# Row maxima of attention scores: a pair of key blocks through a difference, a relu on ScalarE and one sum-and-maximum on VectorE

## The chip, the cores and the metric

The kernel runs on one NeuronCore of a Trainium2 chip. Its engines work side by side, each through its own queue in order: TensorE (PE: matrix products, written to PSUM), VectorE (DVE), ScalarE (ACT), GpSimd (POOL, which reads and writes SBUF alone) and SyncE (SP, which issues DMAs). Engines wait for one another through semaphores. The metric is the time of one execution on the device in microseconds (us); less is better.

## The reference

One pre-norm decoder layer over `x` of 2 x 2048 tokens x 512 features, float32. The part that matters here is self-attention with 16 heads of 32 features:

```python
x = x + _L0_attn_ref(_layernorm(x, axis=-1), W_q, W_k, W_v, W_o)
x = x + _L0_xattn_ref(_layernorm(x, axis=-1), ctx_1024, ctx_1024)   # 77 context rows, gelu between two products
x = x + _L0_ffn_ref(_layernorm(x, axis=-1), weights, scale, bias)   # weights by their sign, scale, bias, clip

# in _L0_attn_ref:
Q = apply_rope(proj(W_q), pos, inv_freq)
K = apply_rope(proj(W_k), pos, inv_freq)
V = proj(W_v)
scores = jnp.einsum('bhqd,bhkd->bhqk', Q, K) / jnp.sqrt(jnp.float32(DK))
attn = jax.nn.softmax(scores, axis=-1)
out = jnp.einsum('bhqk,bhkd->bhqd', attn, V)
```

## The kernel before

For each of the two batches `project_batch` makes queries, keys and values, then `Attention.run` walks the attention, and `after_attention` does the rest of the layer for a finished block of 512 queries. `after_attention` is a generator: `background` takes small pieces of it and places them between the steps of the attention (and of the next batch's projection).

**Tiling of the attention.** Features lie on partitions: a group `g` is four heads of 32 rows each. Keys are held in four blocks of 512 (`self.k[0..3]`), queries in four blocks too. A *unit* `u` is 256 queries of one group: 32 units a batch. A unit has eight *steps* i = 0 to 7; step `t = 8 u + i` is the loop variable of `run` (L805). In each step every head of the group handles two chunks of 128 keys (L634: step i takes block i mod 4, its first half of two chunks for i < 4, its second half after that).

**Scores twice.** The exponentials need each query's maximum over all 2048 keys. It is found beforehand: `maxima` (L523) multiplies 128 queries by one block of 512 keys into a PSUM tile `ps` of 128 x 512, queries on partitions, and `reduce` takes the largest of each row with a VectorE reduce (L552) into one element of `mx`, laid out [chunk of queries, head, key block]. One unit's maxima take eight indices (2 chunks of queries x 4 key blocks), and they run 11 steps (`AHEAD`) ahead of the step that carries them. `split_maxima` reduces `mx` over the four blocks, negates it and splits it in three bfloat16 parts (VectorE once, then POOL); `turn_maxima` transposes these on VectorE and sends them through DRAM into `mrow`, as rows. At a unit's start `lower` (L644) puts the negated maximum into the four `st` tiles, and `scores` (L663) adds the products of keys and queries, keys on partitions. For that the `st` tile is not begun anew in every step: to get from one key block to the next, the product with the *difference* of two blocks, `self.dk[kb] = k[kb] - k[kb - 1]`, is added (L660). These differences are made by POOL at the start of a batch (`key_steps`, L600): group 0 at once, groups 1 to 3 as background work.

**One step** (L805 to L843) comes in two halves, heads (0, 1) and heads (2, 3). In the first half TensorE forms maxima products of heads 2 and 3 for step t + 11, interleaved with the score products of heads 0 and 1; ScalarE takes the exponentials of heads 0 and 1 (`pw`, L828); POOL adds their two chunks (`sm`, L830); VectorE reduces the two `ps` tiles. The second half is the same with the pairs of heads exchanged. Then `gather` calls `collect`, for the step before: the products of `pw` and values (`weigh`, L679) and of `sm` and ones (`total`, L693) go to a PSUM tile `acc`, and `acc` is added to the running `num` by VectorE (L712). In two steps of each unit part of that goes otherwise: in step 1 ScalarE copies the values part of `acc` to a new `num` (L716) while VectorE adds the sums part to the previous unit's `num` (L712, 128 x 64), which is then complete, and `divide` takes its reciprocal (L735) and, over the following steps, spreads and multiplies it. In step 2 ScalarE copies the sums part (L721) and VectorE adds the values part.

**Order and buffers.** `run` is under a schedule written by hand for PE, DVE, ACT and POOL: each engine's instructions stand in program order. PSUM has two pools of four buffers. `ps_t` holds the four `st` tiles. `ps_s` holds, in turn, the four `ps` tiles of a step and its `acc`, so five tiles go round in four buffers, and each takes the one that the tile four places earlier has given up: `acc` that of the same step's first `ps` (head 2), and head 1's `ps` that of the `acc` before. Background work takes its PSUM tiles from `ps_s` too while attention runs.

Of the kernel before, what the change touches and what calls it, by code (L numbers as in the profile page):

```python
# [9 lines left out]
F32 = mybir.dt.float32  # L10
F32R = mybir.dt.float32r
BF16 = mybir.dt.bfloat16
AF = mybir.ActivationFunctionType
ALU = mybir.AluOpType
AX = mybir.AxisListType

P = 128
# [4 lines left out]
BLK = 512  # L22
NB = S // BLK
# [6 lines left out]
PART = HQ // SPLIT  # L30
STEPS = NCH // 2
AHEAD = STEPS + 3
SCALE = 1.0 / math.sqrt(DK)
EPS = 1e-5
MAX_VAL = 100.0
# [4 lines left out]
def decoder_layer(  # L40
# [16 lines left out]
    nc = tc.nc  # L57
# [9 lines left out]
    ps_t = ctx.enter_context(tc.tile_pool(name="ps_t", bufs=4, space=bass.MemoryType.PSUM))  # L67
    ps_s = ctx.enter_context(tc.tile_pool(name="ps_s", bufs=4, space=bass.MemoryType.PSUM))
    nums = ctx.enter_context(tc.tile_pool(name="nums", bufs=2))


    def tokens(rows, ch):
# [138 lines left out]
    def project_batch(b, ahead, att, xnt, angles, wk, wq, wv):  # L211
# [15 lines left out]
        def values(ch, xnt, pool=None):  # L227
            pv = (pool or ps_s).tile([P, D], F32, tag="t" if pool else "s", name="pv")
            times(pv, xnt, wv)
            keep_values(ch, pv)  # L230

        def keep_values(ch, pv):
            v = kvq.tile([P, D], F32, tag=f"v{ch}", name=f"v_{b}_{ch}")
            nc.scalar.copy(v, pv)
            att.v.append(v)
# [63 lines left out]
        keep_values(ch - 1, pv)  # L299
        att.lead(AHEAD, 8)  # L300
        values(ch, xnt, ps_t)
# [207 lines left out]
    class Attention:  # L509
        def __init__(self, b):  # L510
            self.b = b
            self.q, self.k, self.v = [], [], []
            self.units = [(qb, g, hf) for qb in range(NB - 1) for g in range(ND) for hf in range(2)]
            self.units += [(NB - 1, g, hf) for hf in range(2) for g in range(ND)]
            self.mx = {}
            self.mrow = {}
            self.num = {}
            self.due = []
            self.st = {}
            self.rows = [slice(h * DK, (h + 1) * DK) for h in range(4)]  # L520


        def maxima(self, n, heads, between=None):  # L523
            u, i = divmod(n, STEPS)
            if u >= NU:
                if between:
                    between()
                return None
            qb, g, hf = self.units[u]
            qc, kb = divmod(i, NB)  # L530
            if u not in self.mx:
                self.mx[u] = small.tile([P, 2, 4, NB], F32, tag="mx", name="mx")
            q0 = hf * HQ + qc * P
            tiles = []
            for h in heads:
                pool, tag = (ps_t, "t") if len(heads) == 4 and h == 3 else (ps_s, "s")
                ps = pool.tile([P, BLK], F32, tag=tag, name="ps")
                nc.tensor.matmul(  # L538
                    ps,
                    self.q[qb][self.rows[h], g, q0 : q0 + P],  # L540
                    self.k[kb][self.rows[h], g, :],
                    start=True,
                    stop=True,
                )
                tiles.append((h, ps))
                if between and h == heads[0]:
                    between()
            mx = self.mx[u]

            def reduce():  # L550
                for h, ps in tiles:
                    nc.vector.tensor_reduce(mx[:, qc, h, kb : kb + 1], ps, AX.X, ALU.max)  # L552

            return reduce

# [44 lines left out]
        def key_steps(self):  # L600
            self.dk = [None] + [
                const.tile([P, ND, BLK], F32, tag=f"w{n}", name=f"dk{n}") for n in "kqv"
            ]
            self.wrap = None

            def differences(g):
                for kb in range(1, NB):
                    nc.gpsimd.tensor_sub(
                        self.dk[kb][:, g, :], self.k[kb][:, g, :], self.k[kb - 1][:, g, :]
                    )  # L610
                    yield False

            def others():
                for g in range(1, ND):
                    for _ in differences(g):
                        for _ in range(4):
                            yield False

            for _ in differences(0):
                pass  # L620
            queue.append(others())
# [141 lines left out]
        def open_block(self, kb):  # L763
            for n in range(AHEAD):
                if n % NB == kb:
                    self.due.append((n, (0, 1, 2, 3)))
# [10 lines left out]
        def run(self):  # L777
# [8 lines left out]
            def gather():  # L786
                nonlocal before
                if prev is not None or before is not None:
                    end = self.collect(prev, before)
                    if end is not None:  # L790
                        ends.append(end)
                before = prev
# [12 lines left out]
            for t in range(NU * STEPS):  # L805
                u, i = divmod(t, STEPS)
                if t == NU * STEPS - AHEAD:
                    free.append(True)
# [9 lines left out]
                for heads, others in (((0, 1), (2, 3)), ((2, 3), (0, 1))):  # L818
                    if i == 0:
# [3 lines left out]
                    reduce = self.maxima(  # L823
                        t + AHEAD, others, lambda: self.scores(u, i, heads, 0)
                    )
                    self.scores(u, i, heads, 1)
                    for h in heads:
                        nc.scalar.activation(pw[:, h], self.st[h], AF.Exp, scale=SCALE)  # L828
                    hs = slice(heads[0], heads[1] + 1)
# [6 lines left out]
                gather()  # L836
                if (t + AHEAD) % STEPS == 0 and u + 1 < NU:
                    self.turn_maxima(u + 1)
                if (t + AHEAD) % STEPS == STEPS - 1 and u + 1 < NU:
                    self.split_maxima(u + 1)  # L840
# [78 lines left out]
```

## Time and profile before

| | us |
|---|---|
| median of 3 runs | 2534.59 (2534.11 to 2536.28) |
| the profiled execution | 2535.18 |
| its span, first to last instruction | 2533.3 |

Busy time and number of the groups that the change touches or that stand beside them:

| line, engine, what | count | busy us | mean ns |
|---|---|---|---|
| L552 VectorE, reduce 128 x 512 to 128 x 1 | 2048 | 1268.1 | 680 |
| L828 ScalarE, exponential 128 x 512 | 2048 | 1062.8 | 603 |
| L830 POOL, sum 128 x 512 | 1024 | 1283.7 | 1274 |
| L712 VectorE, `acc` into `num` (three widths) | 512 | 227.2 | 444 |
| L716 ScalarE, copy of `acc`, 128 x 256 | 64 | 23.9 | 374 |
| L735 VectorE, reciprocal 128 x 64 | 64 | 35.4 | 553 |
| L168 VectorE, statistics of a row | 96 | 65.3 | 684 |

How to read what follows. A group's line gives line of the kernel, engine, operation and tiles. A timeline's line gives start, duration (both in us from the span's start), engine, line, operation, how many of them in a row are merged, and in brackets how long the engine was idle before and what ended that idle time. A line of waits gives who waited for whom, the total in us, how often, and the longest. The chain is followed back from the last instruction to whatever released each one. Durations of instructions in a row overlap: four exponentials of 0.60 us follow one another in 2.07 us. The ends of products are modelled, so a busy TensorE need not be at its peak.

### The profile page before, as it was taken

The page shows a single profiled execution, that of the slowest core. Times are in us where ns is not written, and L with a number is a line of the kernel's source. Part 1 is how long each engine was busy: PE and PEld are TensorE (multiplying, and loading weights), DVE is VectorE, ACT ScalarE, POOL GpSimd, SP SyncE. Part 2 cuts the span into 40 slices and gives each one's busy share as a digit, 9 for nine tenths or more (in the row PEclk, how much of TensorE's full clock was granted, in tenths as well). Part 3 has the DMA queues.
Part 4 walks back from the last instruction along what each step waited for, and adds up shares of the span by engine and source line. Part 5 has one row for each costly group of instructions (what it writes and reads, how often), then busy time and mean ns, then how long its engine had stood idle before and what let it go on. Part 6 is the DMA issues. An engine that isn't in the chain of part 4 may idle for free.

```text
span 2533.3 us, 89869 instructions
## 1 busy us (share of the span) xinstructions
PE 2472.2 (98%) x39268; PEld 1658.7 (65%) x39268; DVE 1835.2 (72%) x3891; ACT 1268.2 (50%) x2457; POOL 1754.6 (69%) x1925
## 2 busy tenths in 40 slices
PE   8999999999999999999999999999999999999898
PEld 4446777666766676666654467776677666766675
DVE  4447888787878787876444488886878787878665
ACT  2113666555656564654521156665556555645463
POOL 2326888678867886787743279785788678867882
PEclk9999999999999999999999999999999999999999
DMA  4000000001000000000211000000000001000100
GB/s 150 21 21 2 3 4 3 3 3 32 8 3 3 27 12 3 3 28 19 73 30 34 9 3 4 3 4 3 11 28 3 3 3 36 3 3 3 36 4 18
DMA packets 37048, 41.87 MB, mean 17 GB/s; under 512 B 19350, under 2 KB 19862, under 8 KB 36656
## 3 DMA queue, kind: packets, MB, share of 16 engines
q1 hardware_dynamic: 36656, 36.14, 4.7%
q8 instruction: 308, 5.05, 0.8%
q14 instruction: 84, 0.69, 0.1%
HBM read 27.23 MB, written 8.90 MB: 14 GB/s over the span
## 4 chain that ended last, share of the span: by engine, by line
PE 88%; DVE 5%; POOL 3%; DMA 2%; ACT 1%; issue 1%; SPq 0%; POOLq 0%; ACTq 0%
PE ps L538 21%; PE acc L679 18%; PE st L663 15%; PE acc L693 8%; PE pk L214 4%; PE pq L214 4%; PE po L446 4%; PE pv L214 4%; DVE mx L552 2%; PE pf L424 2%; POOL sm L830 2%; PE st L644 1%; PE ptqk L222 1%; PE po L472 1%; PE pt L377 1%; DVE st L168 1%
## 5 line engine op out<-in xcount | busy, mean ns | idle before, releaser
L830 POOL TENSOR_TENSOR sm<-pw 128x512 f32<-128x512 f32 x1024 | 1283.7, 1274 | 410.9 <-ACT pw L828 408.0
L828 ACT ACTIVATE pw<-st 128x512 f32<-128x512 f32 x2048 | 1062.8, 603 | 777.1 <-PE ps L538 576.8
L552 DVE TENSOR_REDUCE mx<-ps 128x1 f32<-128x512 f32 x2048 | 1268.1, 680 | 219.2 <-PE ps L538 218.4
L538 PE MATMUL ps<-k,q 32*128 32x512 f32 x4096 | 1054.1, 624 | 0.4 <-DVE mx L552 0.4
L679 PE MATMUL acc<-pw,v 128*32 128x256 f32 x8192 | 551.9, 387 | 5.5 <-DVE mx L552 4.5
L538 PEld LDWEIGHTS ps<-k,q 32*128 32x128 f32 x4096 | 374.4, 185 | 97.4 <-issue 23.9
L679 PEld LDWEIGHTS acc<-pw,v 128*32 128x32 f32 x8192 | 214.9, 109 | 282.0 <-DVE mx L552 180.9
L693 PEld LDWEIGHTS acc<-sm,ones 128*32 128x32 f32 x16384 | 305.0, 110 | 89.5 <-POOL sm L830 1.4
L693 PE MATMUL acc<-sm,ones 128*32 128x64 f32 x16384 | 323.1, 219 | 1.1 <-POOL sm L830 1.1
L712 DVE TENSOR_TENSOR num<-acc,num 128x320 f32<-128x320 f32 (+2 forms) x512 | 227.2, 444 | 101.8 <-PE acc L693 59.3
L663 PE MATMUL st<-q,dkq 32*128 32x256 f32 x2048 | 261.5, 390 | 0.0
L663 PE MATMUL st<-q,dkv 32*128 32x256 f32 x2048 | 255.4, 390 | 0.0
L663 PE MATMUL st<-q,dkk 32*128 32x256 f32 x2048 | 252.6, 388 | 0.0
L250 POOL TENSOR_TENSOR r<-r 128x512 f32<-128x512 f32 x64 | 81.2, 1270 | 151.4 <-DVE r L249 151.4
L663 PEld LDWEIGHTS st<-q,dkq 32*128 32x128 f32 x2048 | 169.8, 184 | 9.3
L663 PEld LDWEIGHTS st<-q,dkk 32*128 32x128 f32 x2048 | 165.1, 184 | 10.0 <-ACT pw L828 0.4
L663 PEld LDWEIGHTS st<-q,dkv 32*128 32x128 f32 x2048 | 164.9, 185 | 8.9 <-ACT pw L828 0.2
L663 PE MATMUL st<-q,k 32*128 32x256 f32 x1024 | 145.7, 401 | 0.0
L663 PE MATMUL st<-q,wrap 32*128 32x256 f32 x1024 | 129.8, 390 | 0.0
L168 DVE BATCH_NORM_STATS2 st<-x 128x6 f32<-128x512 f32 x96 | 65.3, 684 | 84.1 <-DMA x<-in_x_dram 83.9
L223 ACT COPY q<-ptqk 128x512 f32<-128x512 f32 x32 | 18.8, 586 | 203.2 <-PE ptqk L222 203.2
L214 PE MATMUL pk<-wk,xnt 128*128 128x512 f32 x256 | 117.7, 603 | 2.1 <-ACT xnt L206 2.1
(118 smaller groups left out, 2164.3 us busy)
## 6 DMA issues: line engine op xcount, KB each, us to landing
x<-in_x_dram SPq DMA_DIRECT2D x64, 256.0 KB
out_dram<-x SPq DMA_DIRECT2D x32, 256.0 KB
mrow<-rows SPq DMA_DIRECT2D x496, 0.8 KB
wv<-in_wv_t_dram SPq DMA_DIRECT2D x2, 1024.0 KB
wk<-in_wk_t_dram SPq DMA_DIRECT2D x4, 256.0 KB
wq<-in_wq_t_dram SPq DMA_DIRECT2D x4, 256.0 KB
wo<-in_wo_t_dram SPq DMA_DIRECT2D x1, 1024.0 KB
wf<-in_wf_t_dram SPq DMA_DIRECT2D x4, 256.0 KB
```

What stands on the lines that cost most here:

```text
L168: nc.vector.bn_stats(st, xc)
L214: nc.tensor.matmul(dst, xnt[:, i, :], w[:, i, :], start=(i == 0), stop=(i == ND - 1))
L250: nc.gpsimd.tensor_add(r[:, 0, a], r[:, 0, a], r[:, 1, a])
L446: nc.tensor.matmul(ps, ot[:, i, cols], wo[:, i, :], start=(i == 0), stop=(i == ND - 1))
L538: nc.tensor.matmul(ps, self.q[qb][self.rows[h], g, q0 : q0 + P], self.k[kb][self.rows[h], g, :], start=True, stop=True,)
L552: nc.vector.tensor_reduce(mx[:, qc, h, kb : kb + 1], ps, AX.X, ALU.max)
L663: nc.tensor.matmul(self.st[h][:, c, :], keys[r, g, kc * P : (kc + 1) * P], self.q[qb][r, g, hf * HQ : (hf + 1) * HQ], start=False, stop=Tr ...
L679: nc.tensor.matmul(acc[self.rows[h], 0:HQ], self.v[self.chunk(i, c)][:, d0 : d0 + DK], pw[:, h, c, :], start=(c == 0), stop=(c == 1), skip ...
L693: nc.tensor.matmul(acc[self.rows[h], HQ : HQ + PART], ones[:, n, :], sm[:, h, n * PART : (n + 1) * PART], start=(fresh and n == 0), stop=( ...
L712: nc.vector.tensor_add(num[:, part], acc[:, part], num[:, part])
L828: nc.scalar.activation(pw[:, h], self.st[h], AF.Exp, scale=SCALE)
L830: nc.gpsimd.tensor_add(sm[:, hs, :], pw[:, hs, 0, :], pw[:, hs, 1, :])
```

## The change

For two of the four heads, pairs of key blocks are no longer reduced one by one. `PAIRS` names the second block of each pair: for head 1 the pairs are (0, 1) and (2, 3), for head 3 the pair is (1, 2). At the first block of a pair TensorE multiplies the queries with `dk[kb + 1]`, the difference of the two key blocks, in place of the block; ScalarE takes the positive part (relu) of this from PSUM into an SBUF tile `gain`. At the second block TensorE multiplies with the *first* block's keys, and VectorE, in one `tensor_tensor_reduce`, adds `gain` to the scores (written back to `ps`) and takes the maximum of each row: max(a, b) = a + relu(b - a). The element of `mx` that belongs to the first block is not written any more, so `mx` is set to a very low number first. A pair is begun only when the differences of its group have been issued (`self.led`). Heads 0 and 2, and head 3's first and last block, are as before.

```diff
@@ constants @@
+LOWEST = -3.0e38
+PAIRS = {1: (1, 3), 3: (2,)}
...
+    gains = ctx.enter_context(tc.tile_pool(name="gains", bufs=2))
...
@@ Attention.__init__ @@
+            self.gain = {}
+            self.led = set()
...
@@ Attention.maxima @@
             if u not in self.mx:
                 self.mx[u] = small.tile([P, 2, 4, NB], F32, tag="mx", name="mx")
+                nc.vector.memset(self.mx[u], LOWEST)
...
                 ps = pool.tile([P, BLK], F32, tag=tag, name="ps")
+                keys, gain, begun = self.k[kb], None, False
+                if (h, kb) in self.gain:
+                    keys, gain = self.k[kb - 1], self.gain.pop((h, kb))
+                elif g in self.led and kb + 1 in PAIRS.get(h, ()):
+                    keys, begun = self.dk[kb + 1], True
                 nc.tensor.matmul(
                     ps,
                     self.q[qb][self.rows[h], g, q0 : q0 + P],
-                    self.k[kb][self.rows[h], g, :],
+                    keys[self.rows[h], g, :],
                     start=True,
                     stop=True,
                 )
-                tiles.append((h, ps))
+                tiles.append((h, ps, gain, begun))
...
             def reduce():
-                for h, ps in tiles:
-                    nc.vector.tensor_reduce(mx[:, qc, h, kb : kb + 1], ps, AX.X, ALU.max)
+                for h, ps, gain, begun in tiles:
+                    most = mx[:, qc, h, kb : kb + 1]
+                    if begun:
+                        gain = gains.tile([P, BLK], F32, tag="gain", name="gain")
+                        nc.scalar.activation(gain, ps, AF.Relu)
+                        self.gain[h, kb + 1] = gain
+                    elif gain is not None:
+                        nc.vector.tensor_tensor_reduce(
+                            ps, ps, gain, 1.0, LOWEST, ALU.add, ALU.max, most
+                        )
+                    else:
+                        nc.vector.tensor_reduce(most, ps, AX.X, ALU.max)
...
@@ Attention.key_steps, differences @@
+                    if kb == NB - 1:
+                        self.led.add(g)
                     yield False
```

## The prediction

> **What bounds the kernel now.** I read the page first: busy shares, then the chain that ended last.
>
> ```profile
> span 2533.3 us, 89869 instructions
> ...
> PE 2472.2 (98%) x39268; PEld 1658.7 (65%) x39268; DVE 1835.2 (72%) x3891; ACT 1268.2 (50%) x2457; POOL 1754.6 (69%) x1925
> ...
> PE 88%; DVE 5%; POOL 3%; DMA 2%; ACT 1%; issue 1%; SPq 0%; POOLq 0%; ACTq 0%
> ```
>
> TensorE carries the chain. VectorE, which the change unloads, holds 5% of it. Next I took the chain in a stretch of attention with no other work beside it (225 to 455 us), and then the waits.
>
> ```profile
> by line: PE ps L538 31.6%; PE acc L679 29.4%; PE st L663 24.6%; PE acc L693 13.0%; PE st L644 1.5%
> ```
>
> There the chain is TensorE alone, at about 3.38 us a step; VectorE and ScalarE save nothing there by being faster, but can lose by being late. How late they may be is read from the timeline of one unit's second step (i = 1) and third (i = 2). First ScalarE, then VectorE:
>
> ```profile
> 359.31 2.07 ACT L828 ACTIVATE pw<-st 128x512 f32<-128x512 f32 x4 [1.56 <-PE ps L538]
> 361.44 0.37 ACT L716 COPY num<-acc 128x256 f32<-128x256 f32 x1
> 362.69 2.07 ACT L828 ACTIVATE pw<-st 128x512 f32<-128x512 f32 x4 [0.88 <-PE ps L538]
> ```
>
> ```profile
> 359.08 2.48 DVE L552 TENSOR_REDUCE mx<-ps 128x1 f32<-128x512 f32 x4 [0.53 <-PE ps L538]
> 361.85 0.23 DVE L712 TENSOR_TENSOR num<-acc,num 128x64 f32<-128x64 f32 x1 [0.28 <-ACT num L716]
> 362.11 0.55 DVE L735 RECIPROCAL num<-num 128x64 f32<-128x64 f32 x1
> 362.58 2.41 DVE L552 TENSOR_REDUCE mx<-ps 128x1 f32<-128x512 f32 x4
> ```
>
> ```profile
> 363.26 0.42 PE L679 MATMUL acc<-pw,v 128*32 128x256 f32 x4
> ```
>
> The reader is to see a string of four: the addition at L712 starts 0.04 us after ScalarE's copy (361.44 + 0.37), the reciprocal follows, the first reduce of step 2 starts at 362.58, lasts 0.63, and TensorE's value products start 0.05 us after its end, since `acc` takes the PSUM buffer that this reduce frees (four buffers, five tiles a step). TensorE alone would have come there at 361.31 (its first product of the step) + 1.93 (the usual time to that point) = 363.24. So this string ends just where TensorE arrives: no slack. The waits say that it holds in nearly every unit:
>
> ```profile
> DVE num L712 <- ACT num L716: 22.1, 56, 3.0
> ```
>
> VectorE is late only where the previous block's output work runs beside attention, as here, where statistics stand among the reduces:
>
> ```profile
> 533.08 0.68 DVE L168 BATCH_NORM_STATS2 st<-x 128x6 f32<-128x512 f32 x1
> 533.79 0.18 DVE L169 BATCH_NORM_AGGREGATE stats<-st 128x2 f32<-128x6 f32 x1
> 533.89 1.25 DVE L552 TENSOR_REDUCE mx<-ps 128x1 f32<-128x512 f32 x2
> 535.06 0.48 DVE L712 TENSOR_TENSOR num<-acc,num 128x320 f32<-128x320 f32 x1
> 535.46 0.20 DVE L586 STREAM_TRANSPOSE square<-mt 128x32 bf16<-128x32 bf16 x1
> 535.59 0.65 DVE L168 BATCH_NORM_STATS2 st<-x 128x6 f32<-128x512 f32 x1
> 536.27 0.18 DVE L169 BATCH_NORM_AGGREGATE stats<-st 128x2 f32<-128x6 f32 x1
> 536.37 2.45 DVE L552 TENSOR_REDUCE mx<-ps 128x1 f32<-128x512 f32 x4
> ```
>
> This step began on TensorE at 534.09; 1.94 later it was ready for `acc`, but the reduce ended at about 537.0 and `acc` began at 537.08: 1.05 us lost.
>
> **The change, part by part.** *Counts.* Of 2048 reduces 1320 stay. 364 pairs become 364 ScalarE relus, 364 fused operations (TENSOR_TENSOR_REDUCE), and, as the built program shows, 364 small VectorE instructions behind these that write `mx` 128x1; 64 memsets of 128x32 come new. TensorE's, POOL's and SP's instructions keep number and order; the products only take `dk` in place of `k`, same shape.
>
> *VectorE.* A reduce costs 0.68 busy and 0.62 in a row of them (four in 2.48). The fused operation is not in the trace. Nearest below: TENSOR_TENSOR of the same shape from PSUM and SBUF, L360, 690 ns. Above: two passes, 680 + 690 = 1.37 us. I take 0.69, since one stream in and out is what that row does. The small write: between LOAD_MASK_SELECT's 13 ns and the 128x1 rows (L179, 158 ns); I take 0.15. The memset: 0.16 (L561). Busy: 728 x 0.68 = 495 off, 364 x 0.84 + 64 x 0.16 = 316 on, so 179 us less. In the pure stretches this is worth nothing: TensorE covers it.
>
> A rule speaks against even this. The Trainium skill, "VectorE: DVE Perf Modes", section "Rules for kernel authors", says that fusing chained VectorE operations does not pay and that their number is what to cut; the same page, under "Two Vector instructions with no wait between them", counts an operation that writes its accumulator as two. By that the number stays (728 against 364 + 364), and the gains below would be nil: 2551. The rows above show 128x1 operations at a quarter of a reduce's time, so I go by durations.
>
> *Gain where VectorE is late.* Key blocks run ahead by 11 steps, so step i of a unit handles index (i + 3) mod 8; a relu replaces a reduce at i = 1, 3, 5, 7 (head 1) and 2, 6 (head 3); i = 0 and 4 keep four VectorE operations. The step before the stall shown is i = 5: one reduce less ahead of the stalled one, 0.6 of 1.05 gained. Two steps on, behind i = 7, a like stall of 0.64 loses a reduce but takes the longer fused operation: 0.5. A stall of 0.16 behind an earlier i = 6 goes whole. One of 0.51 in an i = 2 is then set by the copy string below: 0.3. After i = 0 a stall of 0.14 grows by 0.1. Each occurs in six query blocks: 6 x (0.6 + 0.5 + 0.16 + 0.3 - 0.1) = 8.8 us; at most the whole stalls, 6 x (1.05 + 0.64 + 0.16 + 0.51 - 0.1) = 13.6, at least half of the taken sum, 4, if other waits take over. The stalls of about 0.6 behind the split of the transposed tile (`low`, L399) wait for ScalarE's cast and TensorE's transposes, and stay.
>
> *Loss: the relu ahead of the copy.* At i = 1 ScalarE gets head 1's relu between the four exps and the copy L716. A relu is like L828 (603 ns) or L206 (586); in a row they follow at (2.07 - 0.60) / 3 = 0.49. It starts at about 361.28 and ends at 361.87; the copy, overlapping by 0.1 as the others do, starts at 361.77 in place of 361.44. That is 0.33, and it goes down the string: addition 362.18, reciprocal 362.44, reduce 362.91 to 363.54, `acc` 363.59. VectorE ended a reduce earlier at 361, but stands behind the addition. Queued there are all later reduces, and TensorE waits for the first. Head 1's tile of step 2 needs `acc`'s buffer, free at 362.41, wanted at 362.28: inside the same 0.33. At i = 2 the relu sits between the exps; the copy L721 comes at 365.17, when both TensorE's sums and the exps are done, and step 3 is on pace, even 0.04 better in the pure case. If the relu cost as much as an ACTIVATE with per-partition operands (L369, 820 ns), the delay would be 0.56. Lower: if sums on TensorE end later than I read, 0.2.
> Of 62 such places in the timeline, 54 show no work of TensorE's behind the step and a stall under 0.05; two are a batch's first unit (no reciprocal) and two its last (no maxima). The eight others hide it behind longer waits. 50 x 0.32 = 16.0 us.
>
> *Elsewhere.* Other relus end within 0.56 us of the next step's start, and the buffer that they free is wanted at 0.97 (second half), or they end 0.43 before (first half). Exps of heads 2 and 3 come 0.49 later at i = 2 and 6; their tiles are wanted 0.4 later than that. POOL's sums have about a microsecond. `dk` is read eleven steps earlier than before, but only after POOL was given its last difference. All at nothing; without this cover each 0.1 us in every unit costs 6 us. A rule on the choice of engine: the Trainium skill, "ScalarE: Activation LUTs", section "Rules for kernel authors", wants relu on VectorE; L828's 603 against L552's 680 shows no such advantage at this shape, and by the rule the relus would merely go back to an engine that is not the bound here.
>
> *Sum.* 16.0 - 8.8 = +7.2 on the profiled execution's 2535.18 (span 2533.3 and 1.9 around it), 2542.4; the median shown is 0.6 lower, so 2541.8, said as 2542.
>
> **The rivals.** *Faster:* the relu does not reach the copy (the wait at L712 is on something else, or slack that I don't see). For it: VectorE ends earlier in each such step. Against: 56 waits on this copy. 8.8 gained: 2526. It decides if the copy's delay is below 0.02 us. *No change:* delay 0.2 (10 us) against the gains: 2536. *Much slower, VectorE the bound:* the fused operation at 1.37 us. At i = 0 and i = 4 VectorE idles 0.53 and 0.41 us before the next reduce; 0.69 + 0.15 more (and the memset at i = 4) overruns by 0.3 and 0.6, so 62 x 0.9 = 56 us, and the gain at i = 7 goes: about 2600. Against: no row of this shape on VectorE exceeds 0.7 with PSUM in it. *Not what it says:* the pairs don't form; excluded, 364 stand in the built program.
>
> **How the numbers follow.** Forecast 0.62, with its own range from 50 x 0.2 - 13.6 (2531) to 50 x 0.56 - 4 (2559); no change 0.13; faster 0.13; much slower 0.12. The range 2526 to 2560 takes in the first two and half of faster, 0.81, and leaves much slower out. What differs by less than 0.2% (5 us) can't be told from no change: of the forecast 0.12 falls there. So faster 0.13, same 0.25, slower 0.62.
>
> **What would show it.** Right: in pure stretches the time from step 2's first product to `acc` goes from 1.95 to about 2.28, a unit from 27.34 to about 27.65; the copy L716 starts 0.1 before the relu's end; the stall at 534 halves. Wrong: an unchanged unit; a fused operation over 0.8 us; or stalls at i = 1 or 5, which would be VectorE's new length.

## The result, and the profile after

The changed kernel took 2552.13 us (median of 6 runs, 2549.56 to 2554.82) beside 2534.35 us (6 runs, 2530.74 to 2538.67) for the kernel before: +17.8 us, a ratio of 1.0069 [1.0056, 1.0082]. That is slower, and beyond the 0.2% that can be told from no change. The profiled execution's span is 2549.1 us, 15.8 above that of before.

First the same parts of the page as before, for the changed kernel: busy shares, the chain that ended last by engine, and from the groups the two instructions of the fused operation (the sum with maximum, and the read of the accumulator that writes `mx`) and the relu.

```profile
span 2549.1 us, 90320 instructions
...
PE 2488.4 (98%) x39268; PEld 1661.3 (65%) x39268; DVE 1660.2 (65%) x3955; ACT 1436.1 (56%) x2821; POOL 1758.2 (69%) x1925
...
PE 90%; POOL 4%; ACT 2%; DMA 2%; DVE 2%; issue 1%; SPq 0%; POOLq 0%; ACTq 0%
...
L569 DVE CUSTOM_DVE_ANT_0 ps<-ps,gain 128x512 f32<-128x512 f32 x364 | 250.9, 689 | 0.0
L569 DVE DVE_READ_ACCUMULATOR2_ANT mx<- 128x1 f32 x364 | 51.1, 140 | 0.0
L566 ACT ACTIVATE gain<-ps 128x512 f32<-128x512 f32 x364 | 226.7, 623 | 0.0
```

VectorE did get 175 us lighter (1835.2 to 1660.2), and its share of the chain fell from 5% to 2%. The kernel is slower all the same: TensorE has the same 39268 products and holds more of the chain, since it waits within it. Where it waits is seen in the same unit and the same two steps (i = 1 and i = 2) as before. First ScalarE's timeline, then VectorE's, then the line of TensorE's that starts the value products of step 2, whose first product started at 362.10.

```profile
360.10 2.07 ACT L851 ACTIVATE pw<-st 128x512 f32<-128x512 f32 x4 [1.56 <-PE ps L549]
362.02 0.63 ACT L566 ACTIVATE gain<-ps 128x512 f32<-128x512 f32 x1
362.50 0.42 ACT L739 COPY num<-acc 128x256 f32<-128x256 f32 x1
```

```profile
359.87 1.89 DVE L573 TENSOR_REDUCE mx<-ps 128x1 f32<-128x512 f32 x3 [0.53 <-PE ps L549]
362.95 0.23 DVE L735 TENSOR_TENSOR num<-acc,num 128x64 f32<-128x64 f32 x1 [1.20 <-ACT num L739]
363.21 0.55 DVE L758 RECIPROCAL num<-num 128x64 f32<-128x64 f32 x1
363.69 1.22 DVE L573 TENSOR_REDUCE mx<-ps 128x1 f32<-128x512 f32 x2
```

```profile
364.37 1.07 PE L702 MATMUL acc<-pw,v 128*32 128x256 f32 x16
```

VectorE is done with its three reduces at 361.76 (four before), and then stands idle for 1.20 us in place of 0.28: all that the change saves there is spent on waiting for ScalarE's copy, which stands behind the relu and ends at 362.92. Addition, reciprocal and first reduce follow as before, and `acc` begins 364.37 - 362.10 = 2.27 after the step's first product, 0.32 later than the 1.95 of before. The waits of the changed kernel show the same in 62 units (22.1 us in 56 of them before):

```profile
DVE num L735 <- ACT num L739: 73.5, 62, 3.0
```

To place the rest I read, for each of the 488 steps, the time from TensorE's first product to the first value product, and summed what lies more than 0.05 over the usual 1.94 (2.15 in steps that begin with `lower`), by the step's number i. (The prediction's stall of 0.64 stands in a step that begins with `lower` and is counted over 2.26; over 2.15, which most such steps show, it is 0.75. The values set beside it below are counted over 2.26 too, so their differences hold.) Whatever belongs to step i = 2 stands in one column, and so on; the table is used for the experiments too. The column for i = 0 holds the stalls behind the split of the transposed tile, which differ by some microseconds from one profiled execution to another, without a pattern that I found.

| TensorE's waits ahead of `acc`, us | i=0 | i=2 | i=3 | i=4 | i=6 | all |
|---|---|---|---|---|---|---|
| before | 22.2 | 4.4 | 5.9 | 6.8 | 8.0 | 50.2 |
| after | 18.2 | 21.6 | 7.4 | 7.7 | 8.2 | 65.4 |

The total rises by 15.2, the span by 15.8: the table holds nearly all of the loss. Step 2 alone gives 17.2 of it (0.33 over the usual in 52 units, where it was 0.01 before).

Two more things are in it. The stall that the prediction showed, in the step that then began at 534.09, is smaller: that step now has 537.26 for its first product and 539.68 for `acc`, 2.42 in place of 2.99. And a new wait has come, in steps where ScalarE also normalises rows of the previous block (`xn`, L372). ScalarE's timeline of one such step, then TensorE's line that waits:

```profile
500.64 1.08 ACT L851 ACTIVATE pw<-st 128x512 f32<-128x512 f32 x2 [0.64 <-PE ps L549]
501.61 0.81 ACT L372 ACTIVATE xn<-x,stats 128x512 f32<-128x512 f32 x1
502.31 1.08 ACT L851 ACTIVATE pw<-st 128x512 f32<-128x512 f32 x2
503.27 0.61 ACT L566 ACTIVATE gain<-ps 128x512 f32<-128x512 f32 x1
503.74 0.84 ACT L372 ACTIVATE xn<-x,stats 128x512 f32<-128x512 f32 x1
```

```profile
503.94 0.69 PE L549 MATMUL ps<-k,q 32*128 32x512 f32 x1 [0.16 <-ACT gain L566]
```

The relu, fourth in this timeline, ends at 503.88, and TensorE's next `ps` takes the buffer that it frees 0.06 later. That step's `acc` comes 0.44 late. It happens once in each of six query blocks, and a smaller one (0.18) stands in step 4 of five of them. Step 3 of the same five units starts `acc` 0.22 late for another reason: ScalarE's copy of the sums part ends late there (491.58, behind a relu and two exponentials), VectorE's addition behind it ends at 492.11, and TensorE's product takes that buffer at 492.16.

### The profile page after: what moved, and what is told of

Read it like the earlier page. It is cut to its first block, busy times and chain, and to the rows that moved or that the text cites. A ratio compares the mean times of both kernels' runs of the same rounds, so it can differ in the third digit from the quotient of the medians.

```text
span 2549.1 us, 90320 instructions
## 1 busy us (share of the span) xinstructions
PE 2488.4 (98%) x39268; PEld 1661.3 (65%) x39268; DVE 1660.2 (65%) x3955; ACT 1436.1 (56%) x2821; POOL 1758.2 (69%) x1925
## 4 chain that ended last, share of the span: by engine, by line
PE 90%; POOL 4%; ACT 2%; DMA 2%; DVE 2%; issue 1%; SPq 0%; POOLq 0%; ACTq 0%
PE ps L549 22%; PE acc L702 19%; PE st L686 15%; PE acc L716 8%; PE pq L217 4%; PE po L449 4%; PE pk L217 4%; PE pv L217 4%; POOL sm L853 2%; PE pf L427 2%; PE st L667 1%; PE po L475 1%; ACT pw L851 1%; PE ptqk L225 1%; PE ph L456 1%; PE pt L380 1%
## 5 line engine op out<-in xcount | busy, mean ns | idle before, releaser
L851 ACT ACTIVATE pw<-st 128x512 f32<-128x512 f32 x2048 | 1078.7, 605 | 650.6 <-PE ps L549 346.9
L573 DVE TENSOR_REDUCE mx<-ps 128x1 f32<-128x512 f32 x1320 | 848.1, 681 | 235.0 <-PE ps L549 202.0
L549 PEld LDWEIGHTS ps<-k,q 32*128 32x128 f32 x3368 | 366.3, 185 | 92.5 <-issue 23.7
L735 DVE TENSOR_TENSOR num<-acc,num 128x320 f32<-128x320 f32 (+2 forms) x512 | 229.7, 449 | 271.2 <-PE acc L716 138.5
L569 DVE CUSTOM_DVE_ANT_0 ps<-ps,gain 128x512 f32<-128x512 f32 x364 | 250.9, 689 | 0.0
L566 ACT ACTIVATE gain<-ps 128x512 f32<-128x512 f32 x364 | 226.7, 623 | 0.0
L686 PEld LDWEIGHTS st<-q,dkq 32*128 32x128 f32 x2048 | 177.6, 184 | 9.7
L549 PE MATMUL ps<-dkq,q 32*128 32x512 f32 x244 | 136.7, 640 | 0.0
```

The costliest lines, as they stand in the source:

```text
L549: nc.tensor.matmul(ps, self.q[qb][self.rows[h], g, q0 : q0 + P], keys[self.rows[h], g, :], start=True, stop=True,)
L566: nc.scalar.activation(gain, ps, AF.Relu)
L569: nc.vector.tensor_tensor_reduce(ps, ps, gain, 1.0, LOWEST, ALU.add, ALU.max, most)
L573: nc.vector.tensor_reduce(most, ps, AX.X, ALU.max)
L686: nc.tensor.matmul(self.st[h][:, c, :], keys[r, g, kc * P : (kc + 1) * P], self.q[qb][r, g, hf * HQ : (hf + 1) * HQ], start=False, stop=Tr ...
L735: nc.vector.tensor_add(num[:, part], acc[:, part], num[:, part])
```

## The experiments

The theory to test was that the relu costs time by its *place* in ScalarE's queue, ahead of the copies of `acc`. Its rivals: the *amount* of work on ScalarE, the *buffers* (a `ps` tile freed later by the relu than by a reduce), and the *pairs* themselves (fused operation, memset, the products with `dk`). A unit's maxima run 11 steps ahead, so which head and which pair are led decides in which steps the relus stand. The first four runs divide the change by this; each edit is against the changed kernel unless said otherwise.

**Head 3's pair alone.** Its relus stand in steps 2 and 6, none in step 1.

```diff
-PAIRS = {1: (1, 3), 3: (2,)}
+PAIRS = {3: (2,)}
```

> Only head 3's pair is kept (relus in steps 2 and 6, none in step 1). Theory PLACE (the loss comes from the one relu that stands ahead of ScalarE's copy of the values part in step 1): the wait in step 2 falls from 0.33 us to about 0.01 us, time 2534 to 2538 (what remains is ScalarE crowded by normalisations in steps 5 and 6 of a few units). Rival AMOUNT (each of the 364 pairs costs the same, 17.8 / 364 = 0.049 us, by ScalarE's or VectorE's added work): 122 pairs, +6 us, 2540.

2540.26 us against 2531.94, ratio 1.0034 [1.0020, 1.0047]. The number is the rival's, but the wait is not in step 2 (4.4 as before): it is new, in step 3, 17.9 in place of 5.9, 0.2 to 0.26 over the usual in each of some 50 units (its profiled execution, 2547.29, was the longest of seven, so the sum is rather high). ScalarE's, VectorE's and TensorE's timelines around it:

```profile
362.58 1.08 ACT L851 ACTIVATE pw<-st 128x512 f32<-128x512 f32 x2 [0.80 <-PE st L686]
363.55 0.61 ACT L566 ACTIVATE gain<-ps 128x512 f32<-128x512 f32 x1
364.02 1.11 ACT L851 ACTIVATE pw<-st 128x512 f32<-128x512 f32 x2
364.98 0.26 ACT L744 COPY num<-acc 128x64 f32<-128x64 f32 x1
```

```profile
365.34 0.42 DVE L735 TENSOR_TENSOR num<-acc,num 128x256 f32<-128x256 f32 x1 [0.76 <-ACT num L744]
```

```profile
365.82 0.69 PE L549 MATMUL ps<-k,q 32*128 32x512 f32 x1
```

The relu between the exponentials pushes the *second* copy back, that of the sums part (L744). The addition behind it ends at 365.76, and TensorE's product for head 1 starts 0.06 later in the buffer of that `acc`. Two exponentials stand between relu and copy here, and still the relu sets TensorE's time. The view of waits of the kernel before already has this second copy, with 12.7 us in 43 units (L712 for L721), below the line of 22.1 us that the prediction shows. The theory had to be widened from the first copy to both.

**Head 1's first pair alone.** Its relus stand in steps 1 and 5.

```diff
-PAIRS = {1: (1, 3), 3: (2,)}
+PAIRS = {1: (1,)}
```

> Only head 1's pair of blocks 0 and 1 is kept (relus in steps 1 and 5). PLACE: the wait in step 2 stays 0.33 us in about 50 units, +17 us, less about 3 us gained behind step 5 where statistics delay VectorE: 2546 to 2550. AMOUNT: a third of the pairs, +6 us, 2540.

2548.59 us, ratio 1.0052 [1.0029, 1.0075]: a third of the pairs (half of head 1's, none of head 3's) brings nearly the whole loss. Step 2 has 21.6, to the digit what the whole change has. The amount of work on ScalarE can't be it.

**Head 1's second pair alone.** Its relus stand in steps 3 and 7, away from both copies.

```diff
-PAIRS = {1: (1, 3), 3: (2,)}
+PAIRS = {1: (3,)}
```

> Only head 1's pair of blocks 2 and 3 is kept (relus in steps 3 and 7). PLACE: no wait in step 2 beyond 0.01 us, 2532 to 2536. AMOUNT: +6 us, 2540.

2533.08 us, ratio 0.9998 [0.9988, 1.0008]: about as many pairs as in the run before (122 and 120), and no loss. The stall of 0.64 fell to 0.38 in each of six blocks, and in the same blocks a wait of about 0.39 behind `xn` came in step 4 (9.1 in place of 6.8): a gain and a loss of one size.

**The relu after the first copy.** In step 1 the relu is issued behind `gather`, everything else as in the change.

```diff
-            def reduce():
+            def reduce(late=None):
...
-                        nc.scalar.activation(gain, ps, AF.Relu)
+                        if late is None:
+                            nc.scalar.activation(gain, ps, AF.Relu)
+                        else:
+                            late.append((gain, ps))
...
+                    late = [] if i == 1 else None
...
-                        reduce()
+                        reduce(late)
...
                 gather()
+                for gain, ps in late or ():
+                    nc.scalar.activation(gain, ps, AF.Relu)
```

> All pairs as in the change, but in step 1 ScalarE does the copy of the values part first and head 1's relu after it. PLACE: the copy starts 0.33 us sooner and the wait in step 2 goes; the relu ends about 0.4 us later, and the buffer that it frees is wanted at about that time, so up to 0.1 us may come there: 2535 to 2541. AMOUNT: the same work in another place, 2552.

2543.95 us, ratio 1.0043 [1.0028, 1.0058]: some of the loss went, but not what was expected. ScalarE, then TensorE, in this kernel's step 2:

```profile
361.91 0.37 ACT L742 COPY num<-acc 128x256 f32<-128x256 f32 x1
362.18 0.60 ACT L865 ACTIVATE gain<-ps 128x512 f32<-128x512 f32 x1
```

```profile
362.83 0.69 PE L549 MATMUL ps<-k,q 32*128 32x512 f32 x1
```

The copy is on time, but now the relu holds its own `ps` buffer until 362.78, and TensorE's product takes it 0.05 later: 0.17 a unit. And in step 3, where the second copy is late as in the first experiment, the waits rose to 11.5 from 5.9. So the rival with the buffers is right *here*, in step 2 of this kernel. In the change itself the relu of step 1 stands early and the copy late; there a relu's buffer is what TensorE waits for only in the steps with normalisations.

**Both copies on VectorE.** All pairs and relus stay where the change has them; the copies leave ScalarE.

```diff
-                nc.scalar.copy(self.num[step[0]][:, values], acc[:, values])
+                nc.vector.tensor_copy(self.num[step[0]][:, values], acc[:, values])
...
-                nc.scalar.copy(num[:, parts], acc[:, parts])
+                nc.vector.tensor_copy(num[:, parts], acc[:, parts])
```

> All pairs as in the change, and both ScalarE copies of acc (values part in step 1, sums part in step 2) made by VectorE instead. Theory COPIES (the loss is what the relus add ahead of these two copies, and of all that VectorE does behind them; in the change the wait in step 2, 0.33 us, hides the one in step 3, 0.26 us, which head 3's relu alone brings out): both waits go to at most 0.05 us, and 14 to 18 us of the loss with them: 2532 to 2537. Rival BUFFERS (a relu gives a PSUM buffer back later than a reduce did, and that is what TensorE waits for): nothing changes, 2548 to 2552.

2531.9 us against 2531.09, ratio 1.0000 [0.9991, 1.0009]: 364 relus, 364 fused operations, and no loss. Step 2 is back at 4.4 and step 3 at 5.3. What is left cancels: the stall of 1.05 is at 0.49 as in the change, and waits of 0.44 in step 6 and 0.41 in step 4 stand in six blocks each. VectorE, in the place where it had stood idle for 1.20:

```profile
358.25 1.89 DVE L573 TENSOR_REDUCE mx<-ps 128x1 f32<-128x512 f32 x3 [0.53 <-PE ps L549]
360.68 0.42 DVE L739 COPY num<-acc 128x256 f32<-128x256 f32 x1 [0.54 <-PE acc L716]
361.02 0.21 DVE L735 TENSOR_TENSOR num<-acc,num 128x64 f32<-128x64 f32 x1
361.26 0.55 DVE L758 RECIPROCAL num<-num 128x64 f32<-128x64 f32 x1
361.74 1.46 DVE L573 TENSOR_REDUCE mx<-ps 128x1 f32<-128x512 f32 x2
```

It waits for TensorE's sums only (0.54), and copy, addition and reciprocal run one behind the other. The room that the change made on VectorE takes both copies in full.

**The kernel before, and one relu more.** No pairs at all: in step 1 one relu of an `st` tile is put ahead of the copy, and its result goes nowhere.

```diff
@@ against the kernel before, in run @@
                     if reduce:
                         reduce()
+                    if i == 1 and heads[0] == 2 and reduce:
+                        gain = gains.tile([P, 2, HQ], F32, tag="gain", name="gain")
+                        nc.scalar.activation(gain, self.st[3], AF.Relu)
```

> The kernel before, with every reduce in place, and one relu of a score tile (its result is not used) put on ScalarE ahead of the copy of the values part in step 1. COPIES: 0.33 us in step 2 of about 50 units, +16 us: 2547 to 2551. Rival PAIRS (the cost needs the pairs: fused operation, its write to PSUM, or the later buffer): 2532 to 2536.

2546.78 us, ratio 1.0062 [1.0047, 1.0078]: +15.7 us from 62 instructions of 0.63 us. ScalarE's timeline is that of the change without the change:

```profile
359.50 2.07 ACT L829 ACTIVATE pw<-st 128x512 f32<-128x512 f32 x4 [1.55 <-PE ps L539]
361.43 0.63 ACT L836 ACTIVATE gain<-st 128x512 f32<-128x512 f32 x1
361.91 0.42 ACT L717 COPY num<-acc 128x256 f32<-128x256 f32 x1
```

Step 2 has 21.8. With the run before this settles the cause of the loss in step 2 from both sides: the relu ahead of the copy brings it without the pairs, and the pairs without a copy behind a relu don't.

**The positive part on VectorE.** ScalarE is as before the change; VectorE takes both operations of each pair.

```diff
-                        nc.scalar.activation(gain, ps, AF.Relu)
+                        nc.vector.tensor_scalar(gain, ps, 0.0, None, ALU.max)
```

> All pairs as in the change, the positive part taken by VectorE (a maximum with 0) instead of ScalarE. COPIES: ScalarE's copies are as early as before, VectorE does 0.14 us more a pair than before: no wait in steps 2 and 3, the waits behind statistics a little longer than before: 2533 to 2538. Rival AMOUNT: VectorE has more to do than in the change, so the time rises above 2552.

2531.89 us, ratio 1.0005 [0.9996, 1.0014]. VectorE is then busier than before the change (1849.5 us, 1835.2 before), since each pair takes a positive part (0.68), the fused operation and its small write in place of two reduces, and yet the loss is gone (+0.8 in the medians in place of +17.8, which can't be told from nothing). Step 2 has 4.4.

**Pairs only where VectorE is late.** The last five runs ask whether the gain that the prediction counted is there. Head 1 is led in one unit of eight and there for the first 128 queries only, so that relus stand in steps 5 and 7 and never near a copy.

```diff
-PAIRS = {1: (1, 3), 3: (2,)}
+PAIRS = {1: (1, 3)}
...
-                elif g in self.led and kb + 1 in PAIRS.get(h, ()):
+                elif g in self.led and u % 8 == 2 and i < NB and kb + 1 in PAIRS.get(h, ()):
```

> Head 1's pairs are begun only in steps 5 and 7 of the units whose maxima follow the statistics (14 pairs in all), so that no relu stands ahead of a copy. COPIES: the waits of 1.05 and 0.64 us fall to about 0.48 and 0.39 us in six places, no other wait grows: 4 to 5 us less than before, 2527 to 2531. Rival (the time won there is lost again in the wait for the maxima's rows at the unit's start): as before, 2532 to 2535.

2530.55 us, ratio 0.9997 [0.9989, 1.0006], the stalls of 1.05 and 0.64 untouched: a miss, the wrong units. The next run had `u % 8 == 3`, and the one after it the same with heads 1 and 3 (`PAIRS = {1: (1, 3), 3: (1, 3)}`).

> As the kernel that begins pairs only behind statistics, but in the next unit of each query block, where the waits of 1.05 and 0.64 us are (the one before had the unit wrong by one and left them unchanged). Theory COPIES: they fall to about 0.48 and 0.39 us in six places, nothing else grows, 4 to 5 us less than before, ratio 0.998. Rival (the gain is lost in the wait for the rows of maxima at the unit's start): ratio 1.000.

> The same units, steps 5 and 7, with pairs of heads 1 and 3 both, so that two of four reduces leave VectorE there and none of the relus stands ahead of a copy of acc. COPIES: the waits fall to about 0.3 and 0.2 us, 7 us less than before, ratio 0.997. Rival (ScalarE, with two relus in a step, gives head 1's buffer back too late): no better than with one head, ratio 0.998.

2535.02 us, ratio 1.0009 [0.9999, 1.0019], and 2536.07 us, 1.0018 [1.0006, 1.0029], against 2533.11. Misses again, and the first can't be told from no change: in the profiles these relus come a unit too early, in the stretch of the normalisations, and the stalls were untouched. But the two runs price the other thing by itself. Step 6 has 11.1 and 14.1 in place of 8.0: 0.44 in each of six blocks with one relu in a step, 0.84 with two. ScalarE in the second of them, and TensorE's wait:

```profile
498.80 1.08 ACT L851 ACTIVATE pw<-st 128x512 f32<-128x512 f32 x2 [0.57 <-PE st L686]
499.77 0.60 ACT L566 ACTIVATE gain<-ps 128x512 f32<-128x512 f32 x1
500.24 0.82 ACT L372 ACTIVATE xn<-x,stats 128x512 f32<-128x512 f32 x1
500.95 1.09 ACT L851 ACTIVATE pw<-st 128x512 f32<-128x512 f32 x2
501.90 0.62 ACT L566 ACTIVATE gain<-ps 128x512 f32<-128x512 f32 x1
```

```profile
502.58 0.69 PE L549 MATMUL ps<-k,q 32*128 32x512 f32 x1 [0.57 <-ACT gain L566]
```

Two relus and a normalisation between the exponentials, and TensorE stands idle for 0.57 until the last relu frees its tile.

With `u % 8 == 4` the relus stand in the steps that hold the statistics. Again one head, then two.

```diff
-                elif g in self.led and kb + 1 in PAIRS.get(h, ()):
+                elif g in self.led and u % 8 == 4 and i < NB and kb + 1 in PAIRS.get(h, ()):
```

> Head 1's pairs in steps 5 and 7 of one unit in eight again, one unit further on: the maxima run eleven steps ahead, so steps 5 to 7 of a unit belong to the maxima of the unit after the next. Theory COPIES: the waits of 1.05 and 0.64 us fall to about 0.48 and 0.39 us in six places, no other grows: 4 to 5 us less than before, ratio 0.998. Rival (lost again in the wait for the rows of maxima at the unit's start): ratio 1.000.

> The same unit and steps with pairs of heads 1 and 3. COPIES: the waits fall to about 0.3 and 0.2 us in six places, 7 us less than before, ratio 0.997. Rival (two relus in a step give head 1's buffer back too late): no better than with one head, ratio 0.998.

One head: 2526.26 us against 2532.1, ratio 0.9973 [0.9964, 0.9981]. Two heads: 2520.94 us, ratio 0.9958 [0.9946, 0.9971]. Both are quicker than the kernel before and than the changed one, with 16 and 32 pairs in place of 364. In six blocks each, the stall of 1.05 became 0.49 and then 0.24, and that of 0.64 became 0.38 and then nothing. VectorE in the two-head kernel, in the step that lost 1.05 before, and the start of TensorE's value products in it (its first product was at 533.89):

```profile
533.10 0.66 DVE L573 TENSOR_REDUCE mx<-ps 128x1 f32<-128x512 f32 x1
534.03 0.49 DVE L735 TENSOR_TENSOR num<-acc,num 128x320 f32<-128x320 f32 x1 [0.28 <-PE acc L716]
534.44 0.20 DVE L607 STREAM_TRANSPOSE square<-mt 128x32 bf16<-128x32 bf16 x1
534.56 0.66 DVE L171 BATCH_NORM_STATS2 st<-x 128x6 f32<-128x512 f32 x1
535.25 0.18 DVE L172 BATCH_NORM_AGGREGATE stats<-st 128x2 f32<-128x6 f32 x1
535.35 0.66 DVE L573 TENSOR_REDUCE mx<-ps 128x1 f32<-128x512 f32 x1
```

```profile
536.07 1.07 PE L702 MATMUL acc<-pw,v 128*32 128x256 f32 x16
```

VectorE now waits for TensorE's sums (0.28) ahead of L735, where it had come late, and `acc` starts 2.18 after the step's first product in place of 2.99.

## Why the prediction was right or wrong

The time lay in the range (2526 to 2560) and the sign was right; the size was not: +7.2 forecast, +17.8 measured. That the range held is in part luck: it was wide because the copy might be delayed longer, and the time came near its upper end because of less gain and of waits that it had no term for. By terms:

*Loss by the relu ahead of the copy: right.* Forecast 50 x 0.32 = 16.0; step 2 shows 21.6 - 4.4 = 17.2, and the relu alone, without the change, 15.7 in the time. Every link is where it was put: relu 0.63 us (taken 0.59), copy begun 0.15 before its end (0.10), addition 0.03 after the copy, front of step 2 at 2.27 (2.28), a unit at 27.66 (27.65). The copy itself takes 418 ns in place of 374. The rivals *faster* and *no change*, which needed a smaller delay, fell with this; *VectorE the bound* fell with the fused operation at 0.69 + 0.14 us, which was the value taken (0.69 + 0.15). VectorE's busy time fell by 175 (179).

*Gain where VectorE is late: right in kind, too large.* Forecast per block 0.6 + 0.5 + 0.16 + 0.3 - 0.1; the profile of the changed kernel has 1.05 to 0.48 (0.57), 0.64 to 0.39 (0.25), 0.16 to 0.14 (nothing) and 0.51 unchanged. That is 6 x 0.84 = 5.0 in place of 8.8, still over the lower bound of 4. Two terms were well off. One is the step that loses a reduce but receives the longer fused operation (0.25 for 0.5). The other is the 0.51: by the prediction's own string, which leaves 0.33, no more than 0.18 of it could go, and in the changed kernel `acc` starts 0.38 after VectorE's reduce there, so that the reduce doesn't hold it; what does was not traced. The stall of 0.14 did not grow. The last two runs show the gain without the loss: -5.8 and -11.2 us.

*"Elsewhere ... All at nothing": the step that failed.* The times of the other relus were taken from pure stretches of attention, where they end 0.41 us before their buffer is wanted. Where the previous block's normalisations (0.81 us) stand in the same ScalarE queue, that cover is gone. In the changed kernel this wait takes 6 x 0.44 = 2.6 us in step 6 and 5 x 0.18 = 0.9 in step 4. Step 3 rose by 1.5, of which 5 x 0.22 = 1.1 is the second copy, below. Together that is 5.0 for which the sum had nothing. The two runs with pairs only in the stretch of the normalisations show the first of these alone (+3.2 and +6.1 in step 6; +1.9 and +3.0 in the medians). The gains had been looked for behind just this background work; the losses had not.

A second cover failed too, at little cost in the change itself. Step 3 was called "on pace" because the copy of the sums came in time; with the relu in step 2 it does not, and by itself this costs some 8 us (head 3's pair alone). In the full change step 2 is late already in most units and hides it; it comes out as the 1.1 us just named, in five units whose step 2 was as late before the change. So undoing the first wait uncovers the second, as the relu behind the copy showed; the effects don't add.

*The sum, corrected:* 17.2 - 5.0 + 5.0 = +17.2, against +15.8 in the span and +17.8 in the medians. It is good to a microsecond or two: in the table step 6 rose by 1.0 more than these terms give, and i = 0 fell by 2.5 more, and neither was traced; 0.4 of step 3's 1.5 wasn't either. The missing 10 us of the forecast are 3.8 of gain not made, 5.0 of waits not seen and 1.2 in the loss.

*The two rules.* By the Trainium skill, "VectorE: DVE Perf Modes", section "Rules for kernel authors", which counts VectorE's operations and sees no profit in fusing, the prediction's estimate was 2551, next to the 2552 measured. The agreement is in the number only: the rule leaves out the gain and has nothing on the new waits, which happened to cancel it; the same operations, put where VectorE is late, made the kernel 0.42% quicker [0.29, 0.54]. The other rule, "ScalarE: Activation LUTs", section "Rules for kernel authors", which puts relu on VectorE, was set aside because durations show no advantage (0.62 on ScalarE, 0.68 on VectorE). As advice for this kernel it was right: the relu on VectorE lost nothing against before (1.0005). Its reason, the rate per element, is not what decided; the queue was.

*Open:* pairs of the first 128 queries in every unit, leaving out only steps 1, 2 and those with normalisations, were not tried; nor was a join of the copies on VectorE with pairs kept out of the normalisations.

## What to carry to other kernels

When an operation moves to a less busy engine, ask not how busy that engine is but what stands behind the new instruction in its queue, and who waits for that: here 62 relus of 0.63 us ahead of a copy cost 16 us, and relus of the same size in steps 3 and 7 none where nothing else stood in ScalarE's queue. Check the slack of every such place also in stretches with background work, since that is where both the gains and the new waits lie. And apply an exchange of this kind only where its engine is late: 32 pairs gained 11 us where 364 lost 18.

## What the runs showed of the hardware

The fused sum and maximum is recorded as two instructions, 689 ns for 128 x 512 with one operand and the result in PSUM, and a read of the accumulator of 140 ns: the main one costs what a plain sum of that shape does (690). A copy of 128 x 256 from PSUM on ScalarE took 374 ns by itself and 418 ns right behind a relu, which it overlapped by 0.15 us. Where a product had to wait for its buffer, TensorE started it 0.05 to 0.06 us after the end of the instruction that freed it, behind VectorE (reduce, addition) and behind ScalarE (relu).
